# Making the inputs of two scans side by side, and moving the last batch's expert blocks and returns one scan earlier

## The chip, the cores and the metric

The kernel runs on one core of a Trainium2 chip. The metric is device time in microseconds (us): the median of several executions of one launch. Beside those runs there is one execution taken by the hardware profiler; the profile and the trace describe that one. The engines are PE (TensorE, matrix products; its weight loads are listed apart as PEld), DVE (VectorE), ACT (ScalarE), POOL (GpSimd) and SP (SyncE, which here only issues DMAs). Each engine runs its own list of instructions in order and waits at semaphores for the others.

## The reference

Four batches of 1024 tokens with 128 features pass two layers. Both layers normalise, scale and shift by a modulation vector of the batch, and add the gated result back to x.

```python
# layer 0: attention with rotary positions, then a mixture of experts, the best 2 of 8
h = _layernorm(x) * (1 + ca) + sa
x = x + ga * _L0_attn_ref(h, ...)          # causal softmax attention, 16 heads
h = _layernorm(x) * (1 + cb) + sb
x = x + gb * _L0_ffn_ref(h, ...)           # sum over 2 experts of combine * (silu(g) * u) @ w2
# layer 1: a selective scan, then experts with limited capacity
h = _layernorm(x) * (1 + ca) + sa
x_conv = silu(causal_conv4(h @ W_in_main) + conv_b);  z = h @ W_in_gate
B_sel, C_sel, delta = x_conv @ W_xproj;  delta = softplus(delta)
h_t = exp(delta * A) * h_{t-1} + delta * B_sel * u_t;   y_t = <h_t, C_sel_t>
x = x + ga * ((y + x_conv * D) * silu(z)) @ W_out
x = x + gb * _L1_ffn_ref(layernorm, ...)   # best 2 of 8, 512 slots per expert, dropped beyond
```

The scan runs along 1024 tokens for each of 128 channels and 16 states, for each batch alone. All arithmetic is in float32.

## The kernel before

x stays in the core's memory as 32 tiles of 128 tokens, 8 for each batch. The first two thirds of the time are attention of layer 0, eight stages (a batch, and a half of the heads), which this change does not touch in the code. Beside attention the expert blocks of batches 0 to 2 are done. What follows, and what is changed, is layer 1's scan stage with all that runs beside it.

**The scans.** The loop at L1189 takes the four batches in turn. A batch's scan has 16 steps `m`; each makes two *recurrences* of 128 rows (8 channels x 16 states) over 512 tokens, the first half of the tokens in steps 0 to 7, the second in 8 to 15. So a scan is 32 recurrences, and the four are 128. One recurrence (`scan`, L898) is a product on PE that spreads `du` to the rows (tile `pu`, L909 through the helper at L46), a multiplication by `bb` on DVE (L911), `da` = exp on ACT (L913), the recurrence itself `h` on DVE (L915) and a multiplication by `cc` on POOL (`hc`, L919). Products `py` on PE gather four `hc` each (`collected`, L922). At the end of a half `scan_output` (L929) multiplies by the gate `sz` (tile `yh`, L932), projects (`pw`), multiplies by a gate on DVE (`wide_gated`, L937) and adds to x on POOL (L939). There are four PSUM buffers for `pu`, three buffers for `da` and for `h`, ten for `hc`, and one for `py`.

**The inputs of a scan.** `scan_inputs(b)` (L840) normalises batch b (statistics on DVE, Ln and Exp and then `xn` on ACT), transposes it (`tp`, PE) to `hT`, makes the convolution as four products into `p1` and `xc` by Silu on ACT (L857), `sz` likewise from `p2` (L860), for two halves; then eight narrow products `pd`, softplus as a chain of small DVE instructions (L815 to L838), `dg` (DVE, L873), `dt` (two PE products, two ACT copies, L880), `du` on POOL (L882), and `bb` and `cc` (four products, four ACT copies, L891). All its PE results share one PSUM buffer, `ps_m` with the tag "m". Batch 0's normalisation and transposition have been done beside attention (`hT0`). Ln, Exp and Silu use different tables on ACT; a change of table is an instruction of its own.

**What runs beside the scans.** A `Beside` (L1164) wraps a generator. In each step from `at` on it is advanced by `n` yields, so that its instructions come into the program between the recurrences; what is left at a scan's end is written out there (`rest`, L1244). The entries are:

- `sort_tokens(3)` in scan 0: routing of batch 3 for layer 0's experts, then 16 scatters of tokens on POOL (L385) into `blocks_in`.
- `first_returns(2)` in scan 0: 16 gathers of expert results on POOL (L287, tile `fy`, six buffers) and their adds to x on DVE (L278).
- `shift_and_scale` at the end of scan 0, small products `rp`.
- `first_blocks(3)` in scan 1: 23 expert blocks of batch 3 (`turn`, `first`, `second` from L409 on; `fye`, L450, is the last DVE instruction of one). They alternate between the PSUM buffers `ps_g` "g" and `ps_m` "d"; "d" is also used by `pw` and by the routing. Weights `fw` and rows come by DMA from SP, and results leave by SP to `blocks_out`.
- `first_returns(3)` in scan 2: it can begin when all blocks have been written.
- `dispatch(b)` (L941), in the scan after b's own: normalises the new x of batch b, routes it and scatters 16 tiles on POOL (L1002) into the slots of layer 1's experts.
- `scan_inputs(b + 1)` in scan b.

After scan 3 the experts of layer 1 run; this change does not touch them.

**What sets the order.** The Python program fixes a priority and, within one PSUM tag or buffer tag, the order in which tiles are given out. A scheduler then lists each engine's instructions when it takes them to be ready, by its own estimate of times. On the chip each list is run strictly in its order, so an instruction that waits holds back all that stand behind it on its engine.

Of the kernel before, what the change touches and what calls it, by code (L numbers as in the profile page):

```python
# [11 lines left out]
F32 = mybir.dt.float32  # L12
# [6 lines left out]
P = 128  # L19
B, S, D = 4, 1024, 128  # L20
NT = B * S // P
TB = S // P
# [6 lines left out]
NCH = 16  # L29
# [20 lines left out]
def adaln_two_layers(ctx: ExitStack, tc: tile.TileContext, I: dict, out: bass.AP):  # L50
# [42 lines left out]
    modT, gate = [], []  # L93
# [217 lines left out]
    def first_returns(b, pool, bufs):  # L311
        _, placei, w = kept[b]
        return return_steps(f_out[b], b * TB, TB, placei, w, pool, bufs)
# [423 lines left out]
    with ExitStack() as es:  # L737
# [99 lines left out]
            nc.vector.scalar_tensor_tensor(dl, s, 2.0, r, ALU.mult, ALU.add)  # L837
            return dl  # L838

        def scan_inputs(b):  # L840

            if b == 0:
                hT = hT0
            else:
                xn = mb.tile([P, TB, D], F32, tag="xn", bufs=1, name="xn")
                yield from norm_steps(b * TB, TB, xn)
                hT = wide("hT", 1, S + 3)
                nc.gpsimd.memset(hT[:, 0:3], 0.0)
                yield from feature_steps(xn, hT[:, 3:], ps_m, modT[1][:, 1, b : b + 1], modT[1][:, 0, b : b + 1])

            xc = wide("xc")
            sz = wide("sz")
            for tok in halves():
                p1 = ps_m.tile([P, 512], F32, tag="m", name="p1")
                for k in range(4):
                    mm(nc, p1, conv_in[:, k, :], hT[:, tok.start + k : tok.stop + k], start=(k == 0), stop=(k == 3))
                nc.scalar.activation(xc[:, tok], p1, AF.Silu, bias=m_cb)  # L857
                p2 = ps_m.tile([P, 512], F32, tag="m", name="p2")
                mm(nc, p2, m_in[:, D:], hT[:, tok.start + 3 : tok.stop + 3])
                nc.scalar.activation(sz[:, tok], p2, AF.Silu)  # L860
                yield

            pd = ps_m.tile([P, TB], F32, tag="m", name="pd")
            for t in range(TB):
                mm(nc, pd[:, t : t + 1], xc[:, t * P : (t + 1) * P], m_dt)
            r = mb.tile([P, TB], F32, tag="sp_r", name="sp_r")
            nc.vector.tensor_copy(r, pd)
            yield
            dl = yield from softplus_steps(r)

            dt = wide("dt")
            dg = mb.tile([P, TB, P], F32, tag="xn", bufs=1, name="dg")
            nc.vector.tensor_mul(  # L873
                dg, ident.unsqueeze(1).to_broadcast([P, TB, P]), dl.unsqueeze(2).to_broadcast([P, TB, P])
            )
            yield
            for g in range(2):
                p1 = ps_m.tile([P, 512], F32, tag="m", name="p1")
                mm(nc, p1, ones, dg[:, 4 * g : 4 * g + 4, :].rearrange("p t q -> p (t q)"))
                nc.scalar.copy(dt[:, g * 512 : (g + 1) * 512], p1)  # L880
            du = wide("du")
            nc.gpsimd.tensor_mul(du, dt, xc)  # L882
            yield

            bc = []
            for name, wt in (("bb", m_B), ("cc", m_C)):
                v = wide(name)
                for tok in halves():
                    p1 = ps_m.tile([P, 512], F32, tag="m", name="p1")
                    mm(nc, p1, wt, xc[:, tok])  # L890
                    nc.scalar.copy(v[:, tok], p1)  # L891
                bc.append(v)
                yield
            return sz, xc, dt, du, *bc
# [286 lines left out]
                    self.take(1)  # L1181
                return self.value

        inputs = Beside(scan_inputs(0), 0, 1)


        sending = None
        output = None
        for b in range(B):  # L1189
            sz, xc, *scanned = inputs.rest()  # L1190
            carry = mb.tile([P, NCH], F32, tag="carry", name="carry")
            beside, among = [], []
            if b == 0:
                beside.append(Beside(first_returns(B - 2, db, 6), 4, 1))
                beside.append(Beside(sort_tokens(B - 1, kept, db, ps_m, "hT2", "hx"), 2, 4))
                beside.append(Beside(shift_and_scale(), NCH - 3, 1))
            if b == 1:
                among.append(Beside(first_blocks(B - 1), 1, 1))
            if b == 2:
                beside.append(Beside(first_returns(B - 1, db, 6), 0, 2))  # L1200
            if sending is not None:
                beside.append(sending)
            if b + 1 < B:
                inputs = Beside(scan_inputs(b + 1), 5 if b == 2 else 2, 3 if b == 2 else 2)
                beside.append(inputs)
            hcs, late = [], None
            for m in range(NCH):

                g, n = divmod(m, NCH // 2)
                hcs += scan([4 * (2 * n % 4 + r) + n // 2 for r in range(2)], g, carry, *scanned)  # L1210
                for f in among:
                    if m >= f.at:
                        f.take(1)
                if n == 1:

                    if late is not None:
                        late()
                        late = None
                        if b + 1 == B:
                            beside.append(Beside(dispatch(b, 0, TB - NL), m + 1, 8))  # L1220
                    elif output is not None:
                        output()
                        output = None
                if n == 2:
                    py = ps_y.tile([P, 512], F32, tag="py", name="py")
                    mm(nc, py, skip, xc[:, g * 512 : (g + 1) * 512], stop=False)
                if n % 2 == 1 and n > 1:
                    collected(n // 2 - 1, hcs[:4], py)
                    hcs = hcs[4:]
                if n == NCH // 2 - 1:  # L1230

                    def late(b=b, g=g, hcs=hcs, py=py, sz=sz):
                        collected(3, hcs, py)
                        scan_output(b, g, py, sz)

                    hcs = []
                for f in beside:
                    if m >= f.at:
                        f.take(f.n)
                for f in among:  # L1240
                    if m >= f.at:
                        f.take(1)
            output = late
            for f in beside + among:  # L1244
                f.rest()
            if b + 1 < B:
                sending = Beside(dispatch(b, 0, TB), 2, 3)
            if b == 1:
                fw_scope.close()
                gw = ctx.enter_context(tc.tile_pool(name="gw", bufs=1, side="right"))  # L1250
                g_w = gw.tile([P, NE, NFC * (P + D)], F32, name="g_w")
                for e in range(NE):
                    nc.sync.dma_start(g_w[:, e, :], I["g_w"][e])
# [163 lines left out]
```

## Time and profile before

| what | us |
|---|---|
| median of 3 runs (2198.32 to 2199.18) | 2198.94 |
| the profiled execution | 2186.78 |
| its span | 2185.1 |
| end of attention's products to the first recurrence of scan 0 | 1424.7 to 1473.8 |
| recurrences of scan 0 | 1473.8 to 1555.3 |
| recurrences of scan 1 | 1588.0 to 1688.8 |
| recurrences of scan 2 | 1693.4 to 1815.3 |
| recurrences of scan 3 | 1850.8 to 1933.7 |
| experts of layer 1 and the end | to 2185.1 |

Times of day in this document are counted from the start of the profiled span. A line of the timeline reads: start, duration, engine, source line, operation, the tile written and the tiles read, the shape, the count, and in brackets the idle time of the engine before it with what ended that idle time. A row of a table of stretches gives for one stretch of time its length and the time in which each engine was busy, with the number of its instructions. A PE instruction counted as busy need not run at full clock; the granted share of the clock is given beside it.

### The profile page before, as it was taken

Reading aid. Unit: us, or ns where it says so; the run is one execution under the profiler, and the core shown is the slowest. Engines: PE = TensorE matmul, PEld = TensorE weight load, DVE = VectorE, ACT = ScalarE, POOL = GpSimd, SP = SyncE. Lnnn points to the kernel's source line nnn. Section 1 sums busy time; section 2 is a strip of 40 time slices with the busy share of each in tenths; the row PEclk is TensorE's granted clock in tenths of the full one; section 3 lists DMA queues with packets and bytes.
Section 4 is the critical chain, followed back from the end, with each engine's and each line's share of the span. In section 5 each row is a group of like instructions: output and inputs, shape, how many; then the busy total and the mean of one; then the engine's idle time right before and its main releaser. Section 6 shows DMA issues by size and latency. Waiting matters only on the chain. (4 is left out here: it accounts for less than half of the span.)

```text
span 2185.1 us, 29044 instructions
## 1 busy us (share of the span) xinstructions
PE 1832.8 (84%) x8957; PEld 972.7 (45%) x8957; DVE 1321.1 (60%) x4001; ACT 939.5 (43%) x2067; POOL 993.6 (45%) x1277
## 2 busy tenths in 40 slices
PE   5399999998999898999988999959698858859784
PEld 3144444454555354455444456523245423227563
DVE  5446566565667755667675566537587785861323
ACT  1145454653454464445374455433564334323221
POOL 1334444346333736523644633244563666571524
PEclk9699999999999998999999999965687757559897
DMA  6300101002222101222200212110121220012425
GB/s 224 126 1 20 30 1 38 12 19 55 72 64 76 48 1 44 77 66 64 77 6 29 69 58 75 35 34 0 35 71 51 75 99 20 1 51 82 131 72 153
DMA packets 103756, 123.59 MB, mean 57 GB/s; under 512 B 15024, under 2 KB 68656, under 8 KB 103600
## 3 DMA queue, kind: packets, MB, share of 16 engines
q1 hardware_dynamic: 84256, 99.01, 15.4%
q0 software_dynamic: 8192, 16.74, 2.5%
q10 hardware_dynamic: 11152, 5.97, 0.9%
q8 instruction: 71, 1.16, 0.2%
q14 instruction: 85, 0.70, 0.1%
HBM read 67.85 MB, written 32.90 MB: 46 GB/s over the span
## 5 line engine op out<-in xcount | busy, mean ns | idle before, releaser
L586 POOL TENSOR_SCALAR pr<-pr,den 128x32 f32<-128x32 f32 (+31 forms) x512 | 353.2, 705 | 301.9 <-DVE den L583 295.8
L580 ACT ACTIVATE pr<-pr,nb 128x32 f32<-128x32 f32 (+31 forms) x512 | 371.6, 727 | 196.9 <-DVE nb L567 193.6
L595 PE MATMUL pt<-ident,pr 128*128 128x128 f32 x2304 | 341.9, 283 | 47.6 <-POOL pr L586 38.1
L46 PE MATMUL sc<-k,q 64*128 64x512 f32 (+14 forms) x1536 | 329.4, 520 | 43.8 <-DVE nb L567 25.3
L595 PEld LDWEIGHTS pt<-ident,pr 128*128 128x128 f32 x2304 | 253.2, 142 | 243.6 <-POOL pr L586 77.4
L46 PE MATMUL po<-pT,v 128*64 128x512 f32 x1152 | 344.7, 621 | 1.8 <-DVE pT L599 1.8
L597 ACT COPY pT<-pt 128x512 f32<-128x512 f32 x288 | 167.7, 582 | 354.9 <-PE pt L595 301.9
L567 DVE CUSTOM_DVE_ANT_0 pr<-sc,mask 128x512 f32<-128x512 f32 (+15 forms) x512 | 272.9, 559 | 73.5 <-PE sc L46 63.9
L599 DVE COPY pT<-pt 128x512 f32<-128x512 f32 x288 | 198.3, 688 | 167.2 <-PE pt L595 154.1
L919 POOL TENSOR_TENSOR hc<-h,cc 128x512 f32<-128x512 f32 x128 | 161.0, 1272 | 127.7 <-DVE h L915 60.2
L46 PEld LDWEIGHTS sc<-k,q 64*128 64x128 f32 x1536 | 122.4, 191 | 198.7 <-DVE nb L567 93.7
L46 PE MATMUL pu<-du,spread 32*128 32x512 f32 x256 | 146.5, 953 | 34.0 <-DVE h L915 30.1
L684 POOL MEMSET pr<- 128x288 f32 x128 | 42.3, 339 | 264.4 <-PE pt L595 260.3
L567 DVE CUSTOM_DVE_ANT_0 pr<-sc,mask,nb 128x416 f32<-128x416 f32 (+15 forms) x256 | 119.9, 496 | 7.0 <-PE sc L46 5.8
L913 ACT ACTIVATE da<-dt,negA 128x512 f32<-128x512 f32 x128 | 91.0, 718 | 75.8 <-DVE h L915 75.5
L911 DVE TENSOR_TENSOR pu<-pu,bb 128x512 f32<-128x512 f32 x128 | 85.9, 686 | 39.9 <-PE pu L46 39.4
L1302 POOL DMA_INDIRECT y<-slots_out,slot x56 | 57.9, 1033 | 108.4 <-PE ph L46 50.7
L46 PEld LDWEIGHTS po<-pT,v 128*64 128x64 f32 x1152 | 69.3, 135 | 84.1 <-issue 42.0
L503 DVE TENSOR_TENSOR rot_w<-proj,sin_sb 128x512 f32<-128x512 f32 x80 | 55.0, 688 | 77.5 <-PE proj L46 44.4
L46 PEld LDWEIGHTS pf<-fxT,fw 128*128 128x128 f32 x552 | 73.5, 202 | 53.6 <-DVE fye L450 15.5
L580 ACT ACTIVATION_READ_ACCUMULATOR pr<-pr,nb 128x1 f32 x512 | 96.3, 188 | 0.0
L545 POOL TENSOR_TENSOR q<-rot_u,rot_v 128x512 f32<-128x512 f32 x64 | 81.3, 1271 | 32.8 <-DMA rot_v<-rot_w 29.1
(273 smaller groups left out, 2714.3 us busy)
## 6 DMA issues: line engine op xcount, KB each, us to landing
fw<-in_f_w SPq DMA_DIRECT2D x92, 320.0 KB, 3.0
rot_v<-rot_w SPq DMA_DIRECT2D x320, 64.0 KB, 2.0
gw<-in_g_w SPq DMA_DIRECT2D x15, 512.0 KB, 5.2
fxe<-blocks_in SPq DMA_DIRECT2D x28, 192.0 KB, 2.6
blocks_out<-fye SPq DMA_DIRECT2D x28, 192.0 KB, 3.0
blocks_in<-mask SPq DMA_DIRECT2D x20, 256.0 KB, 5.2
slots_in<-mask SPq DMA_DIRECT2D x16, 256.0 KB, 4.7
g_w<-in_g_w SPq DMA_DIRECT2D x8, 512.0 KB, 6.4
```

The source lines that it names most:

```text
L46: return nc.tensor.matmul(out, lhsT, rhs, start=start, stop=stop)
L545: nc.gpsimd.tensor_add(to, u.rearrange("p (n q) -> p n q", q=QG), v.rearrange("p (n q) -> p n q", q=QG))
L567: nc.vector.tensor_tensor_reduce(out=pr[hp][:, g, lo:hi], in0=sc[:, hp, : hi - lo], in1=mask[:, MW - hi + lo :] if hi == nk else mask[:, : ...
L580: nc.scalar.activation(p, p, AF.Exp, bias=nb[:, last, hp : hp + 1], scale=-1.0, accum_out=den[:, hp : hp + 1])
L586: nc.gpsimd.tensor_scalar(p, p, den[:, hp : hp + 1], 1.0, ALU.mult, ALU.mult)
L595: next_to(hp == 0 and g == 0, lambda: nc.tensor.transpose(to, p, ident))
L597: nc.scalar.copy(pT[:, hp, :], pt)
L599: nc.vector.tensor_copy(pT[:, hp, :], pt)
L911: nc.vector.tensor_mul(pu, pu, bb[:, tok])
L913: nc.scalar.activation(da, dt[:, tok], AF.Exp, scale=negA[:, c : c + 1])
L919: nc.gpsimd.tensor_mul(hcs[-1], h, cc[:, tok])
L1302: nc.gpsimd.indirect_dma_start(out=y, out_offset=None, in_=yd[k][:, :], in_offset=bass.IndirectOffsetOnAxis(ap=slot[:, k, t : t + 1], axis=0),
```

## The change

1. `scan_inputs` gets the PSUM pool and the tag of its PE results as arguments, and `dg` a buffer of its own in place of the one that it shared with `xn`.
2. Before the first scan the inputs of batches 0 and 1 are made in turn, one yield of each at a time, batch 0 with `ps_m` "m" and batch 1 with `ps_g` "g", until batch 0's are complete. What is left of batch 1's is advanced in scan 0 from step 0, two yields a step.
3. The inputs of batch 2 are advanced in scan 1 and those of batch 3 in scan 2, both from step 0 and by two yields (before: from step 2 by two, and for batch 3 from step 5 by three).
4. `sort_tokens(3)` begins at step 1 of scan 0 (before: 2). `first_blocks(3)` begins at step 13 of scan 0 (before: step 1 of scan 1) and goes on in scan 1 from step 0; in step 10 of scan 1 all that is left of it is written out.
5. `first_returns(3)` begins at step 10 of scan 1 (before: step 0 of scan 2).

```diff
-        def scan_inputs(b):
+        def scan_inputs(b, ps, bank):
...
-                yield from feature_steps(xn, hT[:, 3:], ps_m, modT[1][:, 1, b : b + 1], modT[1][:, 0, b : b + 1])
+                yield from feature_steps(
+                    xn, hT[:, 3:], ps, modT[1][:, 1, b : b + 1], modT[1][:, 0, b : b + 1], tag=bank
+                )
...
-                p1 = ps_m.tile([P, 512], F32, tag="m", name="p1")
+                p1 = ps.tile([P, 512], F32, tag=bank, name="p1")
...
-            dg = mb.tile([P, TB, P], F32, tag="xn", bufs=1, name="dg")
+            dg = mb.tile([P, TB, P], F32, tag="dg", bufs=1, name="dg")
...
-        inputs = Beside(scan_inputs(0), 0, 1)
+        ahead = [Beside(scan_inputs(0, ps_m, "m"), 0, 1), Beside(scan_inputs(1, ps_g, "g"), 0, 2)]
+        while not ahead[0].ended:
+            for f in ahead:
+                f.take(1)
...
+        among = []
         for b in range(B):
-            sz, xc, *scanned = inputs.rest()
+            sz, xc, *scanned = ahead.pop(0).rest()
             carry = mb.tile([P, NCH], F32, tag="carry", name="carry")
-            beside, among = [], []
+            beside = []
             if b == 0:
+                beside += ahead
                 beside.append(Beside(first_returns(B - 2, db, 6), 4, 1))
-                beside.append(Beside(sort_tokens(B - 1, kept, db, ps_m, "hT2", "hx"), 2, 4))
+                beside.append(Beside(sort_tokens(B - 1, kept, db, ps_m, "hT2", "hx"), 1, 4))
+                among.append(Beside(first_blocks(B - 1), NCH - 3, 1))
                 beside.append(Beside(shift_and_scale(), NCH - 3, 1))
             if b == 1:
-                among.append(Beside(first_blocks(B - 1), 1, 1))
-            if b == 2:
-                beside.append(Beside(first_returns(B - 1, db, 6), 0, 2))
+                among[0].at = 0
+                beside.append(Beside(first_returns(B - 1, db, 6), NCH // 2 + 2, 2))
             if sending is not None:
                 beside.append(sending)
-            if b + 1 < B:
-                inputs = Beside(scan_inputs(b + 1), 5 if b == 2 else 2, 3 if b == 2 else 2)
-                beside.append(inputs)
+            if 0 < b < B - 1:
+                ahead.append(Beside(scan_inputs(b + 1, ps_m, "m"), 0, 2))
+                beside += ahead
...
+                if b == 1 and m == NCH // 2 + 2:
+
+                    among.pop().rest()
...
-            for f in beside + among:
+            for f in beside:
                 f.rest()
```

More of the change, by code (lines that the diff above doesn't have):

```diff
@@ L857, in scan_inputs @@
                 nc.scalar.activation(xc[:, tok], p1, AF.Silu, bias=m_cb)
-                p2 = ps_m.tile([P, 512], F32, tag="m", name="p2")
+                p2 = ps.tile([P, 512], F32, tag=bank, name="p2")
                 mm(nc, p2, m_in[:, D:], hT[:, tok.start + 3 : tok.stop + 3])
@@ L861, in scan_inputs @@
                 yield
-            pd = ps_m.tile([P, TB], F32, tag="m", name="pd")
+            pd = ps.tile([P, TB], F32, tag=bank, name="pd")
             for t in range(TB):
@@ L877, in scan_inputs @@
             for g in range(2):
-                p1 = ps_m.tile([P, 512], F32, tag="m", name="p1")
+                p1 = ps.tile([P, 512], F32, tag=bank, name="p1")
                 mm(nc, p1, ones, dg[:, 4 * g : 4 * g + 4, :].rearrange("p t q -> p (t q)"))
@@ L888, in scan_inputs @@
                 for tok in halves():
-                    p1 = ps_m.tile([P, 512], F32, tag="m", name="p1")
+                    p1 = ps.tile([P, 512], F32, tag=bank, name="p1")
                     mm(nc, p1, wt, xc[:, tok])
```

## The prediction

> **What bounds the kernel now.** I read the page's share of busy time first, then the tenths in 40 slices, then sums over stretches cut where a scan begins or ends, and only then the timeline at the cuts.
>
> ```profile
> PE 1832.8 (84%) x8957; PEld 972.7 (45%) x8957; DVE 1321.1 (60%) x4001; ACT 939.5 (43%) x2067; POOL 993.6 (45%) x1277
> PE   5399999998999898999988999959698858859784
> ```
>
> Over the span PE is fullest, but the change touches only slices 27 to 36, where PE's row falls to 5 and 6. So the stage has to be read, not the average. In the windows below (columns: stretch, length, then busy us with instruction count for PE, PEld, DVE, ACT, POOL, then granted PE clock, DMA share, GB/s) the rows are prologue, scan 0, gap, scan 1, the return phase inside scan 2, gap before scan 3, scan 3.
>
> ```profile
> 1424.70:1473.00 48.30, 24.58 (x50) 10.06 (x49) 16.73 (x78) 19.77 (x37) 22.00 (x30) 0.64 0.14 39
> 1473.00:1555.30 82.30, 78.12 (x200) 29.23 (x200) 67.04 (x109) 35.32 (x63) 45.42 (x38) 0.59 0.05 17
> 1555.30:1587.30 32.00, 16.45 (x47) 6.93 (x48) 8.71 (x58) 14.46 (x24) 14.70 (x14) 0.59 0.06 20
> 1587.30:1688.80 101.50, 91.63 (x387) 48.58 (x387) 82.39 (x165) 50.81 (x100) 48.57 (x42) 0.77 0.22 65
> ...
> 1749.80:1785.00 35.20, 13.46 (x30) 4.05 (x26) 28.12 (x54) 9.61 (x17) 28.59 (x24) 0.59 0.41 149
> ...
> 1815.30:1850.10 34.80, 25.63 (x118) 14.20 (x116) 11.89 (x63) 15.32 (x27) 23.46 (x21) 0.82 0.08 27
> 1850.10:1933.70 83.60, 65.88 (x162) 21.45 (x162) 73.18 (x117) 30.15 (x59) 56.64 (x46) 0.57 0.03 10
> ```
>
> A recurrence costs DVE 0.69 (the product, L911) and 1.22 to 1.28 (L915), so 1.93 us; 32 of them make 62 us of each scan. In the gaps DVE, the scan's engine, works 8.7 of 32.0 and 11.9 of 34.8 us: everything waits for the next scan's inputs. In scan 0 PE is full at a clock of 0.59. From 1749.8 to 1785 it is neither; the timeline shows what:
>
> ```profile
> 1747.49 0.26 DVE L450 TENSOR_TENSOR fye<-pf,gate 128x128 f32<-128x128 f32 x1
> 1757.02 0.35 DVE L278 SCALAR_TENSOR_TENSOR x<-fy,f_w,x 128x128 f32<-128x128 f32 x1 [2.83 <-DMA fy<-blocks_out,f_placei]
> 1775.69 7.53 DVE L278 SCALAR_TENSOR_TENSOR x<-fy,f_w,x 128x128 f32<-128x128 f32 x1
> 1783.93 0.33 DVE L278 SCALAR_TENSOR_TENSOR x<-fy,f_w,x 128x128 f32<-128x128 f32 x1
> 1784.29 1.24 DVE L915 TENSOR_TENSOR_SCAN h<-da,carry,pu 128x512 f32<-128x512 f32 x1
> ```
>
> The last expert block ends at 1747.8; its 16 gathers run on POOL, 1.26 us apart, and 16 adds on DVE follow as they land. Of scan 2, 19 recurrences are done before the last add and 13 are left (1784.29 begins the first of them).
>
> **The change, stage by stage.** I take where each instruction lands from the order in which the two built programs list each engine's instructions, since the diff does not give it: engines run these lists in order. Recurrences are counted from 0 over all four scans (scan 1 begins at 32).
>
> *Prologue, +17 us.* Batch 1's inputs add 8 transposes, 8 convolution products and so on to PE, which idles half the stretch (24.6 of 48.3): that much is covered. What is not covered is a queue. The list puts batch 2's normalisation on ACT before the first `xc`:
>
> ```profile
> 1446.14 0.69 ACT L857 ACTIVATE xc<-p,m_cb_sb 128x512 f32<-128x512 f32 x1 [3.03 <-PE p L46]
> 1450.60 0.35 DVE L278 SCALAR_TENSOR_TENSOR x<-fy,f_w,x 128x128 f32<-128x128 f32 x1 [1.02 <-DMA fy<-blocks_out,f_placei]
> ...
> 1459.80 1.37 DVE L831 SCALAR_TENSOR_TENSOR sp_s<-sp_s,sp_w 128x8 f32<-128x8 f32 x7
> ```
>
> Batch 2's x is complete only at the last add, 1450.95. Then statistics (0.6), Ln (0.2), a table load (1.28), Exp (0.2), five small DVE steps (1.0), two xn (0.9) and the Silu table (1.28) put the first `xc` at 1456.6 instead of 1446.1: +10.5. Behind it wait both second halves, p2, pd and so all of softplus. Interleaved xn, xc and products of batch 1 (xn 0.4 each, a cold product pair 2.1) add 4.5 before pd; a table change each way (2 x 1.28) and batch 1's pd (3.1) between the two dt copies add 2. Estimate +17, so the first recurrence at 1491 (was 1473.8). Ends: +12 if batch 1's share fits into holes, +21 if PE stays cold. The norm of batch 1 moves into attention, where PE is full (18.96 of the last 20.7 us) and DVE and ACT are half idle: 0, at most 3.
>
> *Scan 0, +3.5.* PE loses batch 1's transposes, convolution and p2 there (8 us) and gains its dt, B and C (4 x 2.08 + 2 x 2.07) plus the row products. Listing PE's work until recurrence 31 with the row's cold durations (pair of pu 2.0, py 1.9, p 2.07, fpl 3.5, fpin 3.9) gives 82 us; the same list of before gives 74, where 78.12 were measured. A rule speaks to this.
>
> ```profile
> 1478.89 2.08 PE L46 MATMUL pu<-du,spread 32*128 32x512 f32 x4
> 1480.90 2.08 PE L46 MATMUL p<-xc,m_C_sb 128*128 128x512 f32 x2
> ```
>
> PE is busy without a hole from 1480 to 1500 and the granted clock there is 0.50. The Trainium skill, "TensorE: Matmul & The Clock Gate", Part 1, says that about 3.4 us of sustained work lifts the clock to full. By that rule p would cost 1.1, as it does in a warm stretch, PE would need about 50 us and DVE (69 us: 62 for the recurrences and 7 for routing and outputs) would set scan 0 at some 72, 13 below what I take. The row decides: PE's 82 and some 3 until DVE has followed, 85 from the first recurrence to the last, against 81.5 (1473.8 to 1555.3).
>
> *Gap between scans 0 and 1, -32.7.* All inputs of scan 1 stand before recurrence 18 in the lists, so this gap (1555.3 to 1588.0) goes.
>
> *Scan 1, +5.* Scan 1 starts at 1576 (was 1588.0). It has no blocks at first: the 16 scatters of sorted tokens stand one after each pair of POOL products until recurrence 42, so blocks start at recurrence 49 (was 39), at about 1613 (was 1600). Sixteen recurrences with cold PE take 38. Then at recurrence 61 four queues lock: on POOL the output add of scan 0's second half and `du` of batch 2 stand before the products; `du` needs PE's dt products, which stand behind `pw` of that output; `pw` shares bank "d" with the blocks and was asked for after block 7. Between the pu products 63 and 64 PE has 5 block firsts, 12 py, B, C and dt, some 30 us. I count 73 us from 1613 to recurrence 64: 1686.5 (was 1693.4). Scan 1's stretch up to there: 110.5 for 105.4. Ends: 95 if blocks fill the waits, 125.
>
> *Scan 2, +34, the term that decides.* Three facts of the lists. (a) Recurrence 76 is followed on DVE by 6 blocks, the router of dispatch 0, and all 16 return adds; so 13 recurrences are done and 19 left when returns end, instead of 19 and 13: 6 x 2.0 = 12 us more afterwards. (b) Dispatch 0 comes late (its x waits for the `pw` above), so on POOL 11 of its 16 scatters stand among the 16 gathers: 11 x 1.26 = 14. (c) The pile has six blocks in sequence with little beside them: about 25 us for some 13 us of DVE. Walked through: recurrence 76 at 1722, last `fye` at 1750 (was 1747.5), gathers over at 1786, last add at 1790 (was 1784.3), then 19 recurrences, two norms and the routing of dispatch 1, 52 us: end at 1843, so 156 instead of 121.9. One rule gives something back:
>
> ```profile
> 1776.11 2.35 POOL L950 TENSOR_TENSOR hs<-hx,row_scale 128x1024 f32<-128x1024 f32 x1
> 1778.42 2.35 POOL L1012 TENSOR_TENSOR x<-x,gate_bias 128x1024 f32<-128x1024 f32 x1
> 1780.73 2.33 POOL L951 TENSOR_TENSOR hs<-hs,row_shift 128x1024 f32<-128x1024 f32 x1
> ```
>
> The add that takes 7.53 us lies exactly over these three. The Trainium skill, "SBUF — State Buffer", Who interferes with whom, says that a DVE instruction with two SBUF inputs and a POOL instruction that reads SBUF exclude each other. In the new lists the three stand after recurrences 63 and 85, away from the adds, so by the rule 7 us of waiting go; the row alone would let them stay and the end be 1850. I take the rule, since row and rule fit to 0.5 us.
>
> *Gap before scan 3, -4.* It stays: softplus of batch 3 still stands behind recurrence 95. Only conv's first half, its p2 and dispatch 2's 3.5 us of logits leave it. 31 for 35.5. *Scan 3, +1.5* (those logits), *rest 0*: the lists of the tail differ in one load.
>
> Sum: +17 +3.5 -32.7 +5 +34 -4 +1.5 = +24. The profiled execution took 2186.8 (span 2185.1), so 2211; the median of the runs stands 12 above it, 2198.9, and carried over gives **2223**.
>
> **Rivals.** *The gap is won and nothing given back* (the other sign): scans 1 and 2 keep their lengths because blocks fill the waits, so +17 +3.5 -32.7 -4 +1.5 = -15: 2184. For it: DVE has 20 idle us in scan 1. Against: the adds and the POOL scatters in one queue. It decides where scan 2 grows by less than 14. *Cold PE*: the blocks run with more holes; their 92 us of PE work at 0.77 would be 142 at 0.50, 20 more than the walk leaves: 2243. For it: thinner PE work. Against: 128-row products warmed it before. *A wash*: prologue +12, scans +16 instead of +39: about 2197, no change.
>
> **How the numbers follow.** Likeliest 2223: 0.57 (own range 2208 to 2236). Cold 0.22, faster rival 0.14, wash 0.07. A measurement of this kernel tells 0.2% (4.4 us) from no change. So faster 0.14, same 0.07, slower 0.79. The range 2188 to 2252 holds the wash and cold PE and cuts the outer parts of the first and the last.
>
> **What would show it.** First `xc` near 1457 and first recurrence near 1491; no gap at recurrence 32; a hole of PE's pu products of about 30 us before recurrence 64; gathers and slot scatters alternating on POOL; 19 recurrences after the last add; a gap of about 31 before recurrence 96. Wrong if the first `xc` runs before the returns end, or scan 2 stays under 136.

## The result and the profile after

The changed kernel takes 2216.1 us (median of 8 runs, 2211.8 to 2219.5) against 2200.1 (8 runs, 2198.3 to 2209.6) for the kernel before on the same chip: ratio 1.0062, 95% interval 1.0048 to 1.0075. It is slower, as forecast, by 14 to 16 us where 24 were forecast.

The page of the changed kernel, its first line of busy time, and PE's row and that of the granted clock in the 40 slices (tenths):

```profile
PE 1841.8 (83%) x8957; PEld 980.7 (44%) x8957; DVE 1318.1 (60%) x4001; ACT 942.6 (43%) x2069; POOL 996.5 (45%) x1277
PE   5399999998999898999998899868998387859573
...
PEclk9699999999999999999999999977677566559796
```

The averages hardly differ from those of before. What is new is a 3 in slice 32, about 1715 to 1770 us: PE stands still there for the last 27 us of it. The stretches of the same profile, cut at the same events as before (prologue, scan 0, scan 1 up to recurrence 64, scan 2 up to the first return add, the return adds, the rest of scan 2, the gap before scan 3, scan 3; columns: stretch, length, busy us and instructions of PE, PEld, DVE, ACT, POOL, granted PE clock, DMA share, GB/s):

```profile
1430.00:1492.70 62.70, 36.95 (x103) 16.86 (x102) 23.97 (x97) 31.82 (x56) 22.28 (x31) 0.76 0.11 30
1492.70:1566.00 73.30, 63.39 (x212) 22.69 (x211) 67.29 (x102) 30.57 (x61) 50.70 (x46) 0.69 0.06 20
1566.00:1669.60 103.60, 93.89 (x344) 44.38 (x346) 86.48 (x160) 56.16 (x101) 55.26 (x47) 0.76 0.22 63
1669.60:1743.00 73.40, 59.13 (x216) 37.48 (x216) 43.89 (x107) 16.76 (x41) 28.78 (x24) 0.63 0.29 91
1743.00:1771.20 28.20, 0.00 (x0) 0.00 (x0) 8.47 (x30) 0.00 (x0) 21.79 (x23) 0.55 0.34 114
1771.20:1827.70 56.50, 49.05 (x138) 18.76 (x138) 43.52 (x84) 34.91 (x56) 35.50 (x26) 0.65 0.01 3
1827.70:1857.60 29.90, 19.35 (x62) 9.77 (x62) 12.70 (x59) 12.31 (x22) 21.48 (x18) 0.67 0.08 27
1857.60:1944.40 86.80, 73.64 (x182) 24.57 (x180) 69.67 (x118) 31.17 (x61) 58.58 (x48) 0.52 0.03 10
```

The row 1743 to 1771 is the one to look at: no PE, no ACT, DVE busy 8.5 of 28.2 us, and POOL 21.8 us, with 0.3 us between most of its instructions. DVE's timeline there, with the last block's result, a return add that waits, the last add, and the first recurrence after it:

```profile
1731.81 0.29 DVE L450 TENSOR_TENSOR fye<-pf,gate 128x128 f32<-128x128 f32 x1 [0.56 <-PE pf L46]
...
1754.77 0.35 DVE L278 SCALAR_TENSOR_TENSOR x<-fy,f_w,x 128x128 f32<-128x128 f32 x1 [3.64 <-DMA fy<-blocks_out,f_placei]
...
1770.18 0.35 DVE L278 SCALAR_TENSOR_TENSOR x<-fy,f_w,x 128x128 f32<-128x128 f32 x1 [1.02 <-DMA fy<-blocks_out,f_placei]
1773.63 1.22 DVE L917 TENSOR_TENSOR_SCAN h<-da,pu 128x512 f32<-128x512 f32 x1 [3.09 <-POOL hc L921]
```

The recurrence at 1773.63 is number 77; number 76 ended at 1700.3. And POOL in the same time, where gathers (`fy`, L287) and scatters of dispatch 0 (`slots_in`, L1004) take turns:

```profile
1746.85 0.97 POOL L287 DMA_INDIRECT fy<-blocks_out,f_placei  x1 [0.30 <-issue]
1748.13 0.95 POOL L287 DMA_INDIRECT fy<-blocks_out,f_placei  x1 [0.30 <-DVE ln_st L146]
1749.38 1.02 POOL L1004 DMA_INDIRECT slots_in<-hs,desti  x1 [0.30 <-issue]
1750.71 1.00 POOL L1004 DMA_INDIRECT slots_in<-hs,desti  x1 [0.30 <-issue]
1752.02 0.98 POOL L287 DMA_INDIRECT fy<-blocks_out,f_placei  x1 [0.31 <-issue]
```

Eight scatters stand between the first gather (1737.85) and the last (1767.50).

### The profile page after: what moved, and what is told of

Read it like the earlier page. It is cut to its first block, busy times and chain, and to the rows that moved or that the text cites. A ratio compares the mean times of both kernels' runs of the same rounds, so it can differ in the third digit from the quotient of the medians.

```text
span 2212.9 us, 29054 instructions
## 1 busy us (share of the span) xinstructions
PE 1841.8 (83%) x8957; PEld 980.7 (44%) x8957; DVE 1318.1 (60%) x4001; ACT 942.6 (43%) x2069; POOL 996.5 (45%) x1277
## 4 chain that ended last, share of the span: by engine, by line
PE 35%; DVE 10%; issue 5%; POOL 5%; ACT 4%; DMA 3%; another core or an unknown queue 2%; SPq 0%; POOLq 0%; ACTq 0%; DVEq 0%
PE po L46 5%; PE pt L595 5%; PE pf L46 3%; PE pu L46 3%; DVE h L917 3%; PE sc L46 2%; PE ph L46 2%; PE ypy L46 2%; PE pw L46 2%; PE p L46 2%; ACT pr L580 2%; DVE pr L567 2%; PE py L46 1%; POOL pr L586 1%
## 5 line engine op out<-in xcount | busy, mean ns | idle before, releaser
L913 DVE TENSOR_TENSOR pu<-pu,bb 128x512 f32<-128x512 f32 x128 | 85.5, 687 | 29.7 <-PE pu L46 29.4
L46 PEld LDWEIGHTS pf<-fxT,fw 128*128 128x128 f32 x552 | 77.8, 212 | 55.2 <-ACT fxT L417 17.1
L46 PE MATMUL pf<-fxT,fw 128*128 128x128 f32 x552 | 93.2, 311 | 6.3 <-ACT fxT L417 2.7
```

Source lines behind the costliest of these rows:

```text
L46: return nc.tensor.matmul(out, lhsT, rhs, start=start, stop=stop)
L913: nc.vector.tensor_mul(pu, pu, bb[:, tok])
```

## The experiments

All stages of all profiles first, in us, so that each experiment can be read against it. "Prologue" is from the end of attention's last `po` product to the first recurrence; a gap lies between the last recurrence of one scan and the first of the next; "rest" is what follows scan 3. The last column is the ratio of times to the kernel before on the same chip, with its interval. The kernel before took 2196.7 to 2202.5 on the chips of these experiments, so kernels of different experiments are compared by this ratio and not by their times.

| kernel | attention ends | prologue | scan 0 | gap | scan 1 | gap | scan 2 | gap | scan 3 | rest | time / before |
|---|---|---|---|---|---|---|---|---|---|---|---|
| before | 1422.9 | 50.9 | 81.5 | 32.7 | 100.8 | 4.6 | 121.9 | 35.5 | 82.8 | 251.4 | 1 |
| before, second profile (E) | 1423.5 | 50.6 | 81.6 | 32.7 | 97.0 | 4.5 | 122.9 | 35.4 | 82.9 | 268.2 | |
| after | 1430.2 | 63.2 | 72.5 | 1.2 | 95.1 | 7.4 | 158.0 | 30.7 | 85.9 | 268.6 | 1.0062 (1.0048 to 1.0075) |
| A side by side only | 1422.5 | 51.2 | 81.1 | -0.1 | 108.5 | 10.5 | 119.8 | 34.4 | 83.4 | 266.5 | 0.9938 (0.992 to 0.9956) |
| B blocks, returns only | 1424.7 | 60.9 | 76.0 | 28.1 | 107.8 | 1.8 | 138.5 | 30.8 | 86.2 | 268.8 | 1.0114 (1.0075 to 1.0153) |
| C dg shares xn | 1427.2 | 60.7 | 76.0 | 2.3 | 96.8 | 1.4 | 163.8 | 30.7 | 85.9 | 271.8 | 1.0051 (1.0034 to 1.0067) |
| D pw, dispatch on m | 1423.6 | 63.3 | 72.0 | 1.3 | 90.4 | 35.9 | 100.6 | 39.1 | 91.5 | 275.7 | 0.9985 (0.9966 to 1.0003) |
| F batch 2 at step 2 | 1429.1 | 51.2 | 71.1 | 1.1 | 88.0 | 77.8 | 101.9 | 15.9 | 81.9 | 277.3 | 0.9973 (0.9953 to 0.9993) |
| G = D + F | 1426.7 | 51.0 | 70.5 | 1.4 | 106.9 | 36.3 | 102.0 | 27.7 | 91.3 | 274.7 | 0.9953 (0.9942 to 0.9965) |
| H = G + batch 3 on g | 1427.6 | 51.6 | 73.3 | 1.4 | 106.4 | 37.8 | 122.9 | 1.9 | 97.6 | 275.4 | 0.9964 (0.995 to 0.9977) |
| I pw alone on m | 1430.8 | 63.7 | 71.9 | 1.3 | 94.8 | 6.1 | 91.4 | 97.2 | 87.9 | 272.6 | 1.0069 (1.0045 to 1.0093) |
| J = A + batch 3 on g | 1426.0 | 51.0 | 81.1 | -0.1 | 108.8 | 10.5 | 112.3 | 31.8 | 86.2 | 268.7 | 0.9952 (0.9937 to 0.9967) |
| K = A + sorting at step 1 | 1426.4 | 51.1 | 71.1 | 1.1 | 103.8 | 20.5 | 134.3 | 28.6 | 82.5 | 262.0 | 0.9945 (0.9929 to 0.9962) |
| L = F + batch 3 on g | 1427.5 | 51.5 | 73.8 | 1.1 | 87.8 | 78.1 | 105.9 | 1.1 | 97.6 | 275.1 | 0.9984 (0.9961 to 1.0006) |

### A and B: the two halves of the change

A takes the diff's prologue and the old places of sorting, blocks, returns and later inputs:

```diff
-                among.append(Beside(first_blocks(B - 1), NCH - 3, 1))
...
-                among[0].at = 0
-                beside.append(Beside(first_returns(B - 1, db, 6), NCH // 2 + 2, 2))
+                among.append(Beside(first_blocks(B - 1), 1, 1))
+            if b == 2:
+                beside.append(Beside(first_returns(B - 1, db, 6), 0, 2))
...
-                ahead.append(Beside(scan_inputs(b + 1, ps_m, "m"), 0, 2))
+                ahead.append(Beside(scan_inputs(b + 1, ps_m, "m"), 5 if b == 2 else 2, 3 if b == 2 else 2))
```

> Only the inputs of the first two scans are made side by side (with the buffer of its own for dg, and batch 1's rest advanced in scan 0); sorting, expert blocks, returns and the inputs of batches 2 and 3 stand where they stood before. My theory (the new prologue costs less than the gap it removes, and what makes the changed kernel slower is the place of the blocks and returns in scans 1 and 2): the list has batch 2's normalisation behind the xc of both first batches, so the first recurrence comes at about 1482 (before 1473.8, changed 1493.4); scan 0 takes 73 (before 81.5), there is no gap before scan 1, scan 2 takes about 122 to 130 as before (changed 158), 18 or more of its recurrences are done before the last return add. Sum +9 -9 -31 and at most +8: about 2172 to 2180. Rival (the blocks need their time from the end of sorting on, so scans that begin earlier only wait longer for them): scans 1 and 2 grow by the 25 won, 2197 to 2203.

B is the other half:

```diff
-        ahead = [Beside(scan_inputs(0, ps_m, "m"), 0, 1), Beside(scan_inputs(1, ps_g, "g"), 0, 2)]
-        while not ahead[0].ended:
-            for f in ahead:
-                f.take(1)
+        ahead = [Beside(scan_inputs(0, ps_m, "m"), 0, 1)]
...
-            if 0 < b < B - 1:
-                ahead.append(Beside(scan_inputs(b + 1, ps_m, "m"), 0, 2))
+            if b + 1 < B:
+                ahead.append(Beside(scan_inputs(b + 1, ps_m, "m"), 0 if b else 2, 2))
```

> The other half alone: prologue and first gap as before (inputs of batch 0 alone, then batch 1's within scan 0), but sorting, blocks, returns and the inputs of batches 2 and 3 begin where the changed kernel begins them. My theory: the pile of blocks and 16 return adds behind recurrence 76 and the scatters among the gathers come with these starts, so scan 2 takes about 150 (before 122), the gap before scan 1 stays at about 32; about 2225 to 2235. Rival (the earlier blocks fill the gap, and the pile comes only with two scans' inputs at once): scan 2 at most 130, total 2195 to 2203.

A measured 2189.5, B 2225.3, where the kernel before has 2201.4. So -0.6% and +1.1%, which together make +0.5%, the changed kernel's +0.6% within the intervals. A's gain is half of what was expected: the gap went, but scan 1 and the gap behind it grew by 13.6 (scan 0 stayed at 81.1; K says why), and its rival, that nothing is gained, fell. B lost 10.0 in the prologue, which I had not expected there, and 16.6 in scan 2.

### C and F: what makes the prologue longer

```diff
-            dg = mb.tile([P, TB, P], F32, tag="dg", bufs=1, name="dg")
+            dg = mb.tile([P, TB, P], F32, tag="dg" if b != 1 else "xn", bufs=1, name="dg")
```

> The changed kernel, but the dg of batch 1 shares its buffer with xn as all did before, so batch 2's normalisation cannot be listed before batch 1's dt; in the list the first xc follows the end of attention's work at once. My theory (batch 2's two xn with their two table loads ahead of the first xc, waiting for the last return add, are 10.5 of the 19.6 that the first recurrence comes later): first xc at about 1447 to 1451 in place of 1462 or so, first recurrence at 1482 to 1485 in place of 1493.4, the end 8 to 11 earlier: 2205 to 2208. Rival (the prologue is longer because two batches are interleaved in ACT's and PE's lists): first recurrence at 1490 or later and the time within 3 of the changed kernel's 2216.

C moved only the two `xn`; batch 2's Ln and Exp stayed ahead of the first `xc` in ACT's list, so the text above was wrong about its own kernel. It won 2.5 of the prologue's 12.3. F moves the whole normalisation:

```diff
-                ahead.append(Beside(scan_inputs(b + 1, ps_m, "m"), 0, 2))
+                ahead.append(Beside(scan_inputs(b + 1, ps_m, "m"), 2 if b == 1 else 0, 2))
```

> The changed kernel, but the inputs of batch 2 are advanced from step 2 of scan 1 on (as before the change) and not from step 0. In the list batch 2's Ln, Exp and first xn now stand behind the xc of both first batches (in the run that gave dg back its shared buffer only the xn had moved, the Ln and Exp had stayed ahead). My theory (Ln of batch 2, waiting for the last return add ahead of the first xc, is the whole cost of the new prologue): from the end of attention to the first recurrence 51 to 53 as in the kernel before (changed kernel 63.2). After that the list of scans 1 and 2 has another place for the pile: all blocks from the twelfth on, and the returns, stand at recurrence 64, so scan 1 ends later and scan 2 is short, about 100 to 110; end of scan 3 some 10 to 25 earlier, 2192 to 2206. Rival (the wait is only moved to the interleaved xc and products): 60 or more from the end of attention to the first recurrence, and a time within 5 of 2216.

F's prologue is 51.2, the old 50.9. Its ACT timeline, then that of the changed kernel:

```profile
1448.60 1.28 ACT L859 ACT_TABLE_LOAD   x1
1452.99 0.69 ACT L859 ACTIVATE xc<-p,m_cb_sb 128x512 f32<-128x512 f32 x1 [3.10 <-PE p L46]
```

```profile
1450.46 1.28 ACT L153 ACT_TABLE_LOAD   x1
1459.17 0.21 ACT L153 ACTIVATE ln_r<-ln_ve 128x8 f32<-128x8 f32 x1 [7.42 <-DVE ln_ve L151]
1459.40 1.28 ACT L154 ACT_TABLE_LOAD   x1
...
1462.84 1.28 ACT L859 ACT_TABLE_LOAD   x1
1464.14 0.69 ACT L859 ACTIVATE xc<-p,m_cb_sb 128x512 f32<-128x512 f32 x1
```

In the changed kernel ACT stands 7.42 us at batch 2's Ln, which waits for the statistics behind the last return add at 1458.0, and loads two more tables before the first `xc`. With that gone, two batches side by side cost next to no time in the prologue (A and F 51.2, before 50.9). B, which has the old one-batch prologue and the same normalisation in the same place, pays 10.0 for it. F's time is 0.9973 of before; the pile of blocks and the returns moved to recurrence 64, where a wait of 77.8 now stands.

### D, G and I: the pile, the bank and the returns

```diff
-            pw = ps_m.tile([P, 4, D], F32, tag="d", name="pw")
+            pw = ps_m.tile([P, 4, D], F32, tag="m", name="pw")
```

I is this alone; D also has `tag="m"` for the PSUM tiles of `dispatch`; G is D with F's line.

> The changed kernel, but the projection pw of a scan's output and the PSUM results of dispatch take the bank m (that of the scan inputs) in place of d, which the expert blocks use. Nothing else differs. My theory (pw and dispatch 0 stand behind all blocks in the order in which bank d is given out; that holds up recurrence 77, makes the pile and puts the slot scatters among the gathers): in the lists the returns now stand among recurrences 77 to 80, all 16 scatters of dispatch 0 stand before recurrence 64, ahead of the gathers, and dispatch 0 no longer follows the blocks. The last return add comes about 14 earlier than the changed kernel's, scan 2 takes 125 to 140 in place of 158, though blocks and scatters now stand before recurrence 64 and scan 1 grows by 10 to 20. Total 2195 to 2210. Rival (blocks, returns and adds need their time whatever bank the other products use; only the place of the wait changes): within 4 of 2216 or above.

> The changed kernel with both: pw and dispatch on bank m, and the inputs of batch 2 from step 2 of scan 1. My theory (two separate causes): the 12 of the prologue come on top of what the bank gave: 51 to 53 from the end of attention to the first recurrence, returns among recurrences 70 to 72, and 2180 to 2190 (the bank alone 2197). Rival (the blocks set the end, not the prologue): the scans begin 12 earlier and wait 12 longer at recurrence 64, 2194 to 2199.

> The changed kernel, with only pw on bank m; dispatch stays on d. Batch 2's normalisation stays ahead of the first xc. My theory (recurrence 77 waits in the changed kernel because pw of scan 1's first half was asked for behind all blocks in bank d): in the list all recurrences of scan 2 now stand among the blocks, ahead of the return adds; scan 2 takes 75 to 95 in place of 158. The 16 scatters of dispatch 0 still stand among the gathers and the inputs of batch 3 behind the adds, so the gap before scan 3 grows to 90 to 110, and scan 3 begins at 1840 to 1856 (changed 1858): 2198 to 2214. So what the pile costs is not the wait itself but that 19 recurrences stand behind the adds while batch 3's inputs stand behind those. Rival (the pile comes from the returns' own place in step 10 of scan 1, whatever bank pw has): scan 2 at 140 or more with 19 recurrences behind the last add.

D took 2197.0, in the expected range; scan 2 is 100.6, less than expected, and 28.5 of the gain stands again as a wait before recurrence 64. Last block result to last add took 30.8, where it took 38.1 in the changed kernel: without scatters among the gathers that is 7.3 less. D moves other work too, but all 14 profiles agree on the scatters. From the first gather to the sixteenth it takes 21.3 to 23.8 us in the eight profiles with no scatter between them (both of before, A, D, G, H, J, K), 29.7 and 29.8 with eight (the changed kernel, C), and 32.8 to 34.8 with ten (B, F, I, L). G adds F's prologue and comes to 2192.2, between theory and rival. The gains do not add: D and F alone stand 0.0077 and 0.0089 below the changed kernel's ratio, each more than its whole loss of 0.0062, and G stands 0.0109 below.

I is the one that taught most. The pile is gone, as the theory had it: scan 2 lasts 91.4 instead of 158.0, with all 32 recurrences ahead of the adds. The three stretches of I are scan 2, the returns, and the rest of the gap:

```profile
1668.60:1760.00 91.40, 77.48 (x312) 40.24 (x311) 78.47 (x148) 31.64 (x67) 40.86 (x33) 0.72 0.21 62
1760.00:1796.70 36.70, 0.00 (x0) 0.00 (x0) 8.45 (x31) 0.00 (x0) 26.17 (x27) 0.50 0.40 145
1796.70:1857.30 60.60, 39.70 (x115) 19.85 (x116) 20.48 (x95) 20.46 (x39) 32.87 (x27) 0.61 0.06 20
```

But scan 3 begins at 1857.3, where it began at 1858.4, and the ratio is 1.0069 for 1.0062. With the 19 recurrences ahead of the adds the blocks end 21.7 later (1753.8 for 1732.1) and the adds 26.2 later (4.5 of this in the returns, which have ten scatters among them for eight), and batch 3's inputs still need 60.6 after them. So the pile itself was no loss. As I read it, the loss is that three things stand one after the other: blocks with what DVE and PE do beside them, 28 to 37 us of returns in which PE and ACT do nothing, and then either the left recurrences and the inputs or the inputs alone. No run takes one of the three away alone, so this reading is argued and not shown.

### H, J and L: the gap before scan 3

```diff
-                ahead.append(Beside(scan_inputs(b + 1, ps_m, "m"), 2 if b == 1 else 0, 2))
+                ahead.append(Beside(scan_inputs(b + 1, *((ps_m, "m") if b == 1 else (ps_g, "g"))), 2 if b == 1 else 0, 2 if b == 1 else 3))
```

H puts this on G, L on F, J on A. In J alone the program then has the scan's statistics of batch 3 ahead of most of its return adds, so scan 3 is computed from an x without them; the number of instructions is the same.

> As the kernel with bank m and step 2, and besides the inputs of batch 3 take bank g, which is free when the blocks are over, with three yields a step in place of two. In the list the softplus of batch 3 ends at recurrence 89 in place of behind 96. My theory (the gap before scan 3, 31 to 39 in all runs so far, is there because batch 3's inputs share their bank with the output and dispatch that come after recurrence 96): the gap falls below 8, scan 2 grows by at most 15 as that work now runs in it, and the time is 2155 to 2175, less than both kernels. Rival (the inputs of batch 3 need some 55 after the last return add in any case): the gap shrinks by less than 10 and the time is within 8 of the kernel with bank m and step 2.

> The side-by-side inputs of the first two scans alone, as in the first run (2189.5), and besides the inputs of batch 3 on bank g from step 0 of scan 2 by three yields. In the list the adds stand among recurrences 86 to 89, the softplus of batch 3 still at 96. My theory (the gap before scan 3 is the chain from last return add to du, some 51 to 55, less what of scan 2 still runs beside it): as the last add comes at about 1767 and scan 2 ends at about 1795, the gap can fall from 34.4 to 25 to 30 and no further: 2180 to 2187. Rival (the scan before the gap grows by what the gap loses, as where bank g was tried first): within 3 of 2189.5.

> The changed kernel with the inputs of batch 2 from step 2 of scan 1 (2196.5 so) and the inputs of batch 3 on bank g by three yields; pw and dispatch stay on d, and the blocks still pile up at recurrence 64. In the list the softplus of batch 3 ends at recurrence 90 in place of behind 96. My theory (DVE's order decides: with the returns over at recurrence 68 and batch 3's softplus ahead of the last recurrences no stage waits for the next inputs): the gap before scan 3 falls from 15.9 to under 5, scan 2 grows by less than it, 2183 to 2190. Rival (the returns leave so late that the inputs of batch 3 take scan 2's time instead): scan 2 grows from 102 to 114 or more, 2195 to 2200.

In H and L the gap closed (27.7 to 1.9, 15.9 to 1.1), and no time was won: H 2192.6 for 2192.2 on one chip, L 0.9984 of before where F has 0.9973. In J the adds come too late for that; its gap falls by 2.6 only, and its ratio is 0.9952 where A has 0.9938. The expectation of H, 2155 to 2175, was the worst miss. The scans on both sides took the time back: H +20.9 and +6.3, L +4.0 and +15.7 (L's rival had the time right and named scan 2, not scan 3). Part of what L's scan 3 took is POOL's; the group of dispatch's scatters in scan 3 of L, then of F:

```profile
L1004 POOL DMA_INDIRECT slots_in<-hs,desti x20 | 20.0, 1000 | 4.7 <-issue 3.0 <-DVE rank L999 0.7 <-DVE pu L913 0.5
```

```profile
L1004 POOL DMA_INDIRECT slots_in<-hs,desti x8 | 8.0, 999 | 2.3 <-issue 1.4 <-DVE rank L999 0.7
```

Twelve scatters that had run in or before the gap now stand between the `hc` products. The gap had held work, and this work has to go somewhere.

### K and E: scan 0, and the part behind scan 3

```diff
-                beside.append(Beside(sort_tokens(B - 1, kept, db, ps_m, "hT2", "hx"), 2, 4))
+                beside.append(Beside(sort_tokens(B - 1, kept, db, ps_m, "hT2", "hx"), 1, 4))
```

> The side-by-side inputs of the first two scans alone, as in the first run (2189.5), with one thing more of the change: sorting of batch 3 from step 1 of scan 0 in place of step 2. In PE's list the nine fpin products of the sorting then stand behind recurrence 15 with the last C product in place of behind 19. My theory (scan 0 took 72.5 in the changed kernel and 81.1 in the first run because there PE stands at fpin for the routing on DVE, 3.6, and the pu products wait behind it): scan 0 takes 71 to 75, first block end at 1598 to 1604, and the time is 2180 to 2186. Rival (scan 0's length follows the clock that PE is granted, which varies by the stretch, and not the place of sorting): scan 0 at 78 or more, and 2187 to 2192.

Scan 0 as a whole in A and then in K:

```profile
1473.70:1554.80 81.10, 68.30 (x206) 25.45 (x202) 67.06 (x103) 29.74 (x60) 51.15 (x46) 0.65 0.06 17
```

```profile
1477.50:1548.60 71.10, 58.91 (x206) 21.68 (x202) 66.27 (x102) 30.18 (x60) 50.12 (x46) 0.72 0.07 21
```

The same 206 products take PE 9.4 us less, at a granted clock of 0.72 for 0.65, and DVE is left with 4.8 idle us of 71.1. A's timeline shows PE at the routing product, with the `pu` products queued behind it:

```profile
1514.52 0.66 PE L46 MATMUL fpin<-f_both,before 128*128 128x64 f32 x2 [3.64 <-DVE f_both L345]
```

So starting to sort one step earlier wins 10 us in scan 0 (J, with A's order, has 81.1 again). Wait and clock change together, so their shares stay open. The 10 us are not kept: the wait before recurrence 64 and scan 2 grow by 24.5, scan 1 and the last gap lose 10.5, and K's ratio is A's within the intervals. K's 2184.9 us fell into the range of the theory by luck: the kernel before takes only 2196.7 on that chip. At A's 2201.4 the ratio makes 2189, the rival's time; of the theory only the length of scan 0 was right.

E is the kernel before once more, with no edit.

> The kernel before, once more, for a second profile. In the first one the part after scan 3 took 251.4, in the five profiles of changed kernels, which have the same work there, 266.5 to 275.7. My theory (the 251.4 belongs to that one execution, which was 13 below its median): 260 or more after scan 3 and a profiled time of 2193 to 2208. Rival (the part after scan 3 is shorter in the kernel before, and the changed order costs 15 there): 249 to 255 again. The stages up to scan 3 repeat within some 5 either way.

The rest took 268.2 there, so the 251.4 belonged to one execution.

## Why the prediction was right, and where it was not

The direction and the term that decides were right. Two terms of the sum were too high, scan 0 by 12.5 and scan 1 by 8; the prologue was too low by 2.6 and scan 2 by 2.1. Terms of the sum, against the first profile of before:

| step | forecast | measured |
|---|---|---|
| first recurrence | +17 | +19.6: attention's end +7.3, prologue +12.3 |
| scan 0 | +3.5 | -9.0 |
| gap before scan 1 | -32.7 | -31.5 |
| scan 1 up to recurrence 64 | +5 | -3.0 |
| scan 2 | +34 | +36.1 |
| gap before scan 3 | -4 | -4.8 |
| scan 3 | +1.5 | +3.1 |
| rest | 0 | +0.4 against the second profile |
| sum | +24 | +11 in the profiles (+13.6 in the spans against the second profile), +14 to +16 by the medians and the ratio |

**Prologue: right in cause, its parts mis-sized.** From attention's end to the first `xc` it is 33.9 us, before 23.2: the 10.5 for batch 2's normalisation measured 10.7. At the first recurrence it has become 12.0 (the changed kernel less A or F; D less G gives 12.3). The first `xc`, forecast near 1457, is at 1464.1 since attention ends 7.3 later. The 4.5 for interleaving and 2 for the second `pd` are wrong: A pays 0.3 for both. "Attention 0, at most 3" is a little low: the eleven profiles with batch 1's norm inside attention end it at 1422.5 to 1430.8, mean 1427.1, those without at 1422.9, 1423.5 and 1424.7. That this difference is due to the norm was not tested.

**Scan 0: the step that failed.** "The row decides" took every product at its cold duration and made PE the bound with 82. The first half of scan 0 before the change and then after it:

```profile
1473.80:1511.30 37.50, 36.77 (x90) 12.62 (x88) 30.88 (x43) 16.15 (x39) 19.96 (x16) 0.50 0.00 0
```

```profile
1493.40:1532.20 38.80, 33.99 (x127) 12.03 (x126) 35.58 (x61) 19.05 (x44) 22.35 (x17) 0.74 0.00 1
```

The granted clock is 0.74 where 0.50 was assumed; PE does 127 products in 34.0 us, and DVE sets the pace at 35.6 of 38.8. The stage came to 72.5, just what I had worked out from the rule of the Trainium skill, "TensorE: Matmul & The Clock Gate", Part 1, and set aside. The agreement is in part luck: that working had PE at full clock and done in about 50 us, and PE took 63.4 of 73.3 us at 0.69. The rule as stated, full clock after some 3.4 us of sustained work, is still not what the traces show: before, PE was busy 36.8 of 37.5 us and stayed at 0.50. Neither the row of one stretch nor the rule tells the clock of another stretch. What K adds is that the earlier sorting, which was in the diff and to which I gave no price, takes 10 us out of this stage. Without it the side-by-side prologue changes scan 0 by 0.4 only (A 81.1, before 81.5); with it and the old prologue scan 0 is 76.0 (B).

**Gap before scan 1: right,** 31.5 of 32.7; no gap at recurrence 32.

**Scan 1: sign wrong, 8 us off.** The first block result stood at 1608.5, before at 1611.2; I had the blocks start 13 us later than before. Between the `pu` products ahead of recurrence 64 is a hole of 24 us (forecast 30), and the work in it stands in the order forecast, `pw` ahead of the `dt` products (`p<-dg`) and these ahead of the next `pu`:

```profile
1641.84 2.07 PE L46 MATMUL pu<-du,spread 32*128 32x512 f32 x2
...
1645.28 1.74 PE L46 MATMUL pw<-m_out_sb,yh 128*128 128x128 f32 x8
1646.86 1.02 PE L46 MATMUL p<-dg,ones 128*128 128x512 f32 x2
...
1667.06 1.13 PE L46 MATMUL pu<-du,spread 32*128 32x512 f32 x4
```

With `pw` on "d", 12.5 to 16.2 us lie between recurrences 60 and 61 (the changed kernel, C, F, L); with `pw` on "m" it is 0.8 to 2.2 (D, G, H, I). So the bank does make a wait there, though not in every kernel with "d" (before 1.5, A 1.4, B 1.1). But these runs show no price for the four-queue lock: in I recurrence 64 comes only 1.0 earlier (1668.6), and A, which has the blocks in their old place, has a hole of 25 us too. Recurrence 64 came at 1669.6, not 1686.5, since scan 1 had begun 9 earlier (1567.2 for 1576) and its first sixteen recurrences took 33.7, not 38.

**Scan 2, the term that decided: right,** 158.0 for 156. (a) 13 recurrences were done at the last add and 19 left, as counted. In the kernel before, though, 20 were done and 12 left: the one at 1784.29 is the twenty-first of scan 2, not the twentieth. So (a) moves seven recurrences, 14 us at the same price and not 12. From the last add to the end of the scan it took 57.5 (forecast 53). (b) Eight scatters among the gathers, not 11; by D they cost 7.3, not 14. From recurrence 64 to the last `fye` 62.5 (63.5 forecast), from there to the last add 38.1 (40). The kernel before has 54.4, 36.2 and 31.4 for these three parts, so most of the growth, 26, lies behind the last add. What I did not see is that (a) and (c) have no price of their own in this kernel: I takes both away and begins scan 3 at the same time.

**The 7 us given back by the wide POOL operations** were right, and more profiles show it now: where `hs`, `hs` and `x` stand beside the return adds, one add takes 7.53 (both profiles of before), 7.70 (A) or 7.50 (K); where they stand elsewhere and no `hc` is near, as in the changed kernel, C and I, the longest of the 16 takes 0.40, 0.37 and 0.38. What 7 us shorter adds win at the end of the program no run shows by itself. A's DVE line and, from the same profile, its POOL lines:

```profile
1759.38 7.70 DVE L278 SCALAR_TENSOR_TENSOR x<-fy,f_w,x 128x128 f32<-128x128 f32 x1
```

```profile
1758.75 2.35 POOL L952 TENSOR_TENSOR hs<-hx,row_scale 128x1024 f32<-128x1024 f32 x1
1761.05 1.27 POOL L921 TENSOR_TENSOR hc<-h,cc 128x512 f32<-128x512 f32 x1
1762.28 2.34 POOL L953 TENSOR_TENSOR hs<-hs,row_shift 128x1024 f32<-128x1024 f32 x1
1764.59 2.33 POOL L1014 TENSOR_TENSOR x<-x,gate_bias 128x1024 f32<-128x1024 f32 x1
```

The add ends within 0.2 us of the last of four back-to-back POOL operations. That a DVE instruction with two inputs in SBUF, as the add has, and a POOL instruction that reads SBUF exclude each other is what the Trainium skill, "SBUF — State Buffer", Who interferes with whom, says; the trace adds that the add was not held for one of them but for the whole row. `hc` products do the same: in G an add of 3.61 us lies over three of them.

**Rest and rivals.** The rest is 0, as forecast. Of the rivals, "the gap is won" is A, a kernel that leaves the blocks where they were: 0.9938. Cold PE in the blocks did not come: the clock was 0.76 in scan 1; whether the 128-row products kept it there was not tested. The terms of "a wash" sum to -4, 2195 and not 2197; nothing rests on it.

A and K, at 0.9938 and 0.9945 of before, beat both kernels.

## What to carry to other kernels

Take the two halves of a change apart before you judge it: here one wins 0.6% and the other loses 1.1%, and the first alone is the better kernel. An instruction that a scheduler may hoist to the front of an in-order queue is worth a look whenever what it waits for is late: one Ln at the head of ACT's list cost the whole prologue 12 us, and starting its generator two steps later removed it. Before closing a gap, list what runs in it; where PE and DVE were 68 to 89% busy in the scans on both sides and the gap held 7 to 11 scatters (F, G), closing it moved time and won none (L, H).

## What was not expected of the hardware

The part behind scan 3, whose work is the same in each kernel but for a few scatters (13 to 18 are left for it), took from 251.4 to 277.3 us over 14 profiles, and 251.4 and 268.2 in two executions of one kernel. A single pair of profiles therefore misjudges the total by up to some 17 us (27.8 between these two, where the medians differ by 16), while the stages in scans 0 to 3 repeated within 4 us. Stages can be compared from one profile each; totals only from medians.

The clock granted to PE in scan 0 was 0.59 in both profiles of before and 0.69 in the changed kernel. In the changed kernel it was full from 1506.8 to 1520.4 and from 1527.2 to 1537.5; in the first profile of before it stayed at half from 1455.6 to 1530.6. What decides it, these runs do not settle.
